# Register loads once a unit, an earlier dst fetch, and 50 instead of 43 double groups gathered singly in a graph-network kernel

## The chip, the cores and the metric

The kernel runs on one core of one Trainium2 chip. A core has five engines with queues of their own: TensorE (PE, matmuls and their weight loads, PEld), VectorE (DVE), ScalarE (ACT), GpSimd (POOL) and SyncE (SP, which here only issues DMAs). Work on one engine runs in order; engines wait for each other by semaphores. The metric is the device time of one execution in microseconds (us).

## The reference

A graph with 12,500 nodes of 128 features and 400,000 edges with 32 features, sorted by destination. With `h = relu(layernorm(x))`, every edge computes a message from its source, its destination and its own features; the messages are summed per destination, and a GRU cell makes the new node:

```
h   = relu(layernorm(x))
m   = relu([h[src], h[dst], ea] @ w1 + b1) @ w2 + b2      # per edge
agg = segment_sum(m, dst)                                 # per node
gi, gh = agg @ w_ih + b_ih, h @ w_hh + b_hh
r, z = sigmoid(gi_r + gh_r), sigmoid(gi_z + gh_z)
n   = tanh(gi_n + r * gh_n)
out = x + (1 - z) * n + z * h
```

## The kernel before

A first stage (to about 120 us) normalizes all nodes. It leaves `hT_all`, h transposed, 128 features by 12,500 nodes, in SBUF, and `A = h @ w1[0:128]`, one row of 512 bytes per node, in DRAM.

The main loop goes over the edges. 128 edges are a tile, eight tiles a *double group* (k, 391 of them), four tiles, a half of it, a *unit* (u, 782 of them). For a unit the pre-activation is a sum of three parts:

- the edge features and the destination: one matmul per two tiles, `pre` (L592), whose weights are a tile `L` of 64 rows of edge features and 64 rows of a one-hot matrix of the destinations, and whose moving side `RW` holds w1's last rows and a window of 2 x 32 destination rows;
- the source: rows `A[src]`, gathered into `G` by one indirect DMA per tile on POOL (L146), and added by DVE (`add`, L617).

Then ACT applies relu into one of three buffers `RB` (L623), and PE sums the edges by destination (`seg`, L636) through a one-hot `OH` of the destinations. `take` brings the sums from PSUM to SBUF on DVE (`sums`, L644) and ACT (`dcol`, L645). Every 14 double groups a block of 512 nodes goes through the GRU (`node`), a generator whose steps are spread over the following units.

The one-hot in `L` is made by DVE (`onehot_T`, L495) from `Ld`, destination numbers that SP's DMA broadcasts over 64 partitions. `fetch(q)` (L479) asks for the edge features and the destinations of two double groups with three DMAs; in the loop it is called two such fetches ahead. `window(k)` copies the destination window out of `hT_all` (`hw`, L514, DVE) at an address from a register, and multiplies it with w1's middle rows (L517, PE); `window_rows` adds b1 into `RW` (L526, DVE).

Some double groups are not gathered by POOL but *singly*, by a job that is spread over many units beforehand (`mode`, `order`, `SPREAD`): 18 by DVE and 19 by ACT, which copy one column of `hT_all` per edge into a tile `HE` (1024 columns a job; L790 and L788), and 6 by SP, which issues one row DMA of 512 bytes per edge (L795). A column's address stands in a register, so an instruction that loads 32 registers from the index list `at` (L782) stands on the same engine before each 32 columns or rows. A double group of DVE's or ACT's has no gathered rows of A: PE multiplies its columns by w1's first rows (L603), and `add` does nothing for it. `G` has seven buffers for POOL's gathers; a gather into a buffer waits until the last reader of that buffer is done.

The order is written by hand. The loop over units issues, for unit u: the gathers that are due, the fetches, `other(0)`, `take`, `stages(u)` (among them `pre(u+3)`, `add(u+2)`, `relu(u+2)`), `other(1)`, `other(2)`, `seg(u)`, `other(3)`. `other(phase)` runs a share of the live jobs (`run_jobs`), in phase 1 of an even unit `window(k+3)`, in phase 3 `window_rows(k+3)` and a step of `node`. A job is a generator: `run_jobs` takes as many steps (4 columns, or 2 rows) as are due by the share of its span that has passed, and a load comes wherever 32 are used up, so its place among the other instructions changes from unit to unit. The jobs of an engine follow each other: the first starts at unit 30, and each ends a few units before its double group is used.

Of the kernel before, what the change touches and what calls it, by code (L numbers as in the profile page):

```python
# [8 lines left out]
F32 = mybir.dt.float32  # L9
# [12 lines left out]
GRP = 4  # L22
# [5 lines left out]
V = 32  # L28
# [14 lines left out]
PLACE = 20  # L43
CH = PLACE * PAIR
LOAD = 32
STEP = {"act": 4, "dve": 4, "sp": 2}
SPREAD = {"act": 19, "dve": 18, "sp": 6}
NR = 12672

H_AT = 16512  # L50
# [6 lines left out]
def tile_gnn(ctx: ExitStack, tc: tile.TileContext, x, src, srcT, dstT, dstP, eaT, eaP, w1, b1, w2T, b2,  # L57
# [26 lines left out]

    mode, order = {}, {m: [] for m in SPREAD}
    for m, n in SPREAD.items():
        lo = JOBS0 + 15
        for i in range(n):
            k = lo + int((i + 0.5) * (NP - 2 - lo) / n)
            while k in mode:  # L90
                k += 1
            mode[k] = m
            order[m].append(k)
# [385 lines left out]
    def fetch(q):  # L479
        if q * QP >= NP:  # L480
            return
        n = min(QP, NP - q * QP)
        Ls[q] = p3.tile([128, QP * 512], F32, name="L")
        c = slice(q * QP * 512, (q * QP + n) * 512)
        nc.sync.dma_start(Ls[q][2 * V:, :n * 512], eaP[:, c])
        Ds[q] = p3.tile([2 * V, QP * 512], I32, name="Ld")
        for a in range(2):
            nc.sync.dma_start(Ds[q][V * a:V * (a + 1), :n * 512],
                              dstP[a:a + 1, c].to_broadcast([V, n * 512]))

    def onehot_T(k):
        if k >= NP:
            return
        c = slice((k % QP) * 512, (k % QP + 1) * 512)
        nc.vector.tensor_scalar(Ls[k // QP][:2 * V, c], Ds[k // QP][:, c], node_of[:, k:k + 1],  # L495
                                None, op0=ALU.is_equal)


    bases, PB_ = {}, {}

    def window(k):
        if k >= NP:
            return
        b = k // BP
        if k % BP == 0:
            n = min(BP, NP - k)
            _, vals = nc.values_load_multi_w_load_instructions(
                base_i[0:1, b, 0:n], engines=[ET.DVE], min_val=0, max_val=LAST,
                skip_runtime_bounds_check_because="clamped above")
            for i, v in enumerate(vals):  # L510
                bases[k + i] = v
        hw = p3.tile([128, 2, V], F32, name="hw", bufs=2)
        s = hT_all[:, bass.ds(bases.pop(k), V + SHIFT)]
        nc.vector.tensor_copy(hw, bass.AP(tensor=s.tensor, offset=s.offset,  # L514
                                          ap=[list(s.ap[0]), [SHIFT, 2], [1, V]]))
        PB_[k] = ps2.tile([128, 512], F32, name="oh")
        nc.tensor.matmul(PB_[k][:2 * V, :D], hw.rearrange("p a v -> p (a v)"), w1b,  # L517
                         start=True, stop=True)

    def window_rows(k):  # L520
        if k >= NP:
            return
        pm = PB_.pop(k)
        for a in range(2):
            s = slice(V * a, V * (a + 1))
            nc.vector.tensor_tensor(RW[k % 4][s, a, :], pm[s, :D], b1b[s, :], op=ALU.add)  # L526
# [80 lines left out]
    def add(u):  # L607
        if u >= NU:
            return
        if u in HE or u // 2 in hand:  # L610
            RT[u] = PP.pop(u)
            HE.pop(u, None)
            if u % 2:
                hand.pop(u // 2, None)
        else:
            RT[u] = unit(u)
            nc.vector.tensor_tensor(RT[u], PP.pop(u), RT[u], op=ALU.add)  # L617

    def relu(u):
        if u >= NU:  # L620
            return
        o = RB[u % 3]
        nc.scalar.activation(o[:, :, :D], RT.pop(u), AF.Relu)  # L623
        if u % 2:
            G.pop(u // 2, None)
# [142 lines left out]
        nc.sync.dma_start(at[r:r + 1, :], src[t0 * 128:(t0 + PAIR) * 128].rearrange(  # L768
            "(o e) -> o e", o=1))

    def one_by_one(m, k):
        et = {"act": ET.Activation, "dve": ET.DVE, "sp": ET.SP}[m]
        r = by_hand.index(k)
        if m == "sp":
            G[k] = pj[0].tile([128, GRP, 2, D], F32, name="G_sp", bufs=1)
            rows = G[k].bitcast(U8)
        else:
            hand[k] = pj[0].tile([128, PAIR * 128], F32, name=f"HE_{m}")
            he = hand[k].bitcast(U8)
        for e0 in range(0, PAIR * 128, LOAD):  # L780
            low, high = (0, ROW * (N - 1)) if m == "sp" else (H_AT, H_AT + 4 * (N - 1))
            _, vals = nc.values_load_multi_w_load_instructions(  # L782
                at[r:r + 1, e0:e0 + LOAD], engines=[et], min_val=low, max_val=high,
                skip_runtime_bounds_check_because="src holds numbers of nodes")
            for i, v in enumerate(vals):
                e = e0 + i
                if m == "act":
                    nc.scalar.copy(he[:, e * 4:e * 4 + 4], h_bytes[:, bass.ds(v - H_AT, 4)])  # L788
                elif m == "dve":
                    nc.vector.tensor_reduce(he[:, e * 4:e * 4 + 4],  # L790
                                            h_bytes[:, bass.ds(v - H_AT, 4), None],
                                            AX.X, ALU.max)
                else:
                    a, j = divmod(e // 128, GRP)
                    nc.sync.dma_start(rows[e % 128:e % 128 + 1, j, a, :],  # L795
                                      A_bytes[bass.ds(v, ROW)].rearrange("(o f) -> o f", o=1))
                if i % STEP[m] == STEP[m] - 1:
                    yield


    jobs = {}
    for m, kl in order.items():
        start = 2 * JOBS0
        for k in kl:
            end = 2 * k - (8 if m == "sp" else 4)
            jobs.setdefault(start, []).append((m, k, end - start))
            start = end if m != "sp" else 2 * k + 2
    live = {}

    PH = 4  # L810

    def run_jobs(u, phase):
        if u == 2 * JOBS0 and phase == 0:
            early.close()
            pj.append(late.enter_context(tc.tile_pool(name="pj", bufs=2, side="right")))
        if phase == 0:
            for m, k, span in jobs.get(u, ()):
                live[m] = [one_by_one(m, k), u, span, PAIR * 128 // STEP[m], 0]
        for m, job in list(live.items()):
            it, start, span, steps, done = job  # L820
            want = -(-steps * ((u - start) * PH + phase + 1) // (span * PH))
            while job[4] < want:
                job[4] += 1
                if next(it, "end") == "end":
                    del live[m]
                    break


    asked = [RAW]
# [9 lines left out]

    gathers(0)  # L840
    for q in range(2):
        fetch(q)
    for k in range(3):
        window(k)
        window_rows(k)


    def stages(u):
        if u + 7 >= 0:
            raw_stats(u + 7)  # L850
        if u + 6 >= 0:
            raw_fin(u + 6)
            raw_h(u + 6)
        if u % 2 == 0:
            onehot_T(u // 2 + 3)
        elif u > -7:
            onehot(u // 2 + 3)
        if u + 4 >= 0:
            raw_turn(u + 4)
        if u + 3 >= 0:  # L860
            pre(u + 3)
        if u + 2 >= 0:
            add(u + 2)
            relu(u + 2)

    for u in range(-7, 0):
        stages(u)
# [12 lines left out]
    for u in range(NU):  # L880
        k, h = divmod(u, 2)
        gathers(u)
        if h == 0:
            if k % QP == 0:
                fetch(k // QP + 2)
            if k % BP == 0 and k:
                nodes_left.append([node(k // BP - 1), 0])
            if k % PLACE == 1:
                indices(k // PLACE + 2)
            if k % PLACE == 5:  # L890
                place(k // PLACE + 1)
                dst_tile(k // PLACE + 2)
            if k == NP - 20:
                check_windows()
        for r in range(2 * u, min(2 * u + 2, NJ)):
            job_indices(r)
        if u == 2 * JOBS0 - 2:
            nc.vector.tensor_scalar(at, at, place_of[:, 0:1], place_of[:, 1:2],
                                    op0=ALU.mult, op1=ALU.add)

        def other(phase):
            run_jobs(u, phase)
            if h == 0 and phase == 1:
                window(k + 3)
            if h == 0 and phase == 3:
                window_rows(k + 3)
            if phase == 3:
                step(nodes_left)

        other(0)  # L910
        if h == 0:
            take(k - 1)
        stages(u)
        other(1)
        other(2)
        seg(u)
        if u == 0:
            node_setup()
        other(3)
# [173 lines left out]
```

## Time and profile before

| what | value |
|---|---|
| median of 3 runs | 3710.21 us (3707.43 to 3713.02) |
| the profiled execution | 3701.45 us, its span 3699.7 us |
| granted TensorE clock, mean | 0.779 |
| POOL gathers | 2781, 958 ns from A, 0.30 us between |
| DVE columns and register loads | 18,432 and 576 |
| ACT columns and register loads | 19,456 and 608 |
| SP rows and register loads | 6,144 and 192 |
| chain that ended last | the last node block alone, from 3692.57 us on |

A group's line gives the source line, the engine, the operation, the tile written and the tile read, how often it ran, its busy time, the mean ns of one, and then the idle time of the engine just before it, with what ended that idle time. "issue" means that no wait is shown: the engine's own sequencer had not yet handed over the instruction. Register loads, semaphore instructions and the issuing of DMAs run on the sequencers and are not in the busy time. A line of stretches gives the stretch, its length, busy us and count for PE, PEld, DVE, ACT and POOL, then the granted clock, the busy share of the DMA engines and GB/s. A line of waits gives the waiting engine, tile and line, what it waited for, the us in total, the times, and the longest. In a timeline a line is a run of like instructions: start, length, engine, line, what, how many, and in brackets the idle time before the first.

### The profile page before, as it was taken

The numbers are of one execution on the slowest core, as the hardware profiler recorded it, in microseconds if no ns is written. First come the engines' busy times: TensorE is split into PE (matmuls) and PEld (weight loads), VectorE is DVE, ScalarE is ACT, GpSimd is POOL, SyncE is SP. The second block draws the span as 40 slices with busy tenths as digits, with TensorE's granted clock in tenths as the row PEclk, the third lists the DMA queues.
The fourth block names the chain that finished last, engine by engine and source line by source line (L and its number), as shares of the span: only waits on it lengthen the run. The fifth ranks groups of instructions, "written<-read, shape, count | busy, mean of one in ns | idle before, by whom it ended". The sixth has DMA issues, their size and how long they took to land. (4 is left out here: it accounts for less than half of the span.)

```text
span 3699.7 us, 94893 instructions
## 1 busy us (share of the span) xinstructions
PE 2649.8 (72%) x13578; PEld 1639.6 (44%) x13578; DVE 2627.5 (71%) x22515; ACT 2513.9 (68%) x20936; POOL 2663.7 (72%) x2789
## 2 busy tenths in 40 slices
PE   6685665667776777677677777766776777677768
PEld 6453333444443444344444444444444444344435
DVE  7765556677777677767777776777777777777774
ACT  5455556677677777767776776777777777777772
POOL 7677646477777677777777777777777677777775
PEclk9897777778787777778777877878777778787779
DMA  6333222233333333333333333333333333333332
GB/s 202 83 91 82 75 66 75 72 90 85 89 85 90 81 87 88 86 86 87 88 91 83 91 87 88 83 90 87 89 88 94 80 92 88 88 89 87 88 87 65
DMA packets 157886, 325.92 MB, mean 88 GB/s; under 512 B 65057, under 2 KB 77132, under 8 KB 157255
## 3 DMA queue, kind: packets, MB, share of 16 engines
q0 software_dynamic: 88992, 182.43, 19.5%
q1 hardware_dynamic: 68119, 137.33, 13.7%
q14 instruction: 519, 4.25, 0.4%
q8 instruction: 112, 1.84, 0.2%
q10 hardware_dynamic: 144, 0.07, 0.0%
HBM read 305.74 MB, written 13.84 MB: 86 GB/s over the span
## 5 line engine op out<-in xcount | busy, mean ns | idle before, releaser
L146 POOL DMA_INDIRECT G<-A,src_i x2704 | 2589.9, 958 | 980.1 <-issue 770.2
L788 ACT COPY HE_act<-hT_all 128x4 uint8 x19456 | 1966.1, 189 | 583.2 <-issue 580.6
L790 DVE TENSOR_REDUCE HE_dve<-hT_all 128x4 uint8 x18432 | 1336.4, 146 | 716.0 <-issue 707.4
L592 PE MATMUL pre<-RW,L 128*128 128x256 f32 x3128 | 1151.4, 497 | 129.8 <-DVE G L617 95.7
L592 PEld LDWEIGHTS pre<-RW,L 128*128 128x128 f32 x3128 | 685.8, 243 | 439.0 <-issue 287.0
L517 PE MATMUL oh<-w1b,hw 128*64 128x128 f32 x782 | 209.4, 358 | 875.7 <-DVE hw L514 862.5
L636 PE MATMUL seg<-RB,OH 128*32 128x129 f32 x6250 | 645.4, 341 | 0.0
L623 ACT ACTIVATE RB<-G 128x512 f32<-128x512 f32 x676 | 424.7, 628 | 323.2 <-DVE G L617 85.2
L517 PEld LDWEIGHTS oh<-w1b,hw 128*64 128x64 f32 x782 | 89.7, 162 | 1030.2 <-DVE hw L514 997.1
L617 DVE TENSOR_TENSOR G<-pre,G 128x512 f32<-128x512 f32 x676 | 461.0, 682 | 10.1 <-PE pre L592 0.3
L636 PEld LDWEIGHTS seg<-RB,OH 128*32 128x32 f32 x6250 | 351.0, 131 | 239.3 <-issue 134.4
L526 DVE TENSOR_TENSOR RW<-oh,b1b 32x128 f32<-32x128 f32 x782 | 217.7, 278 | 48.2 <-PE oh L517 39.8
L495 DVE TENSOR_SCALAR L<-Ld,node_of 64x512 f32<-64x512 int32 x391 | 192.4, 492 | 83.3 <-DMA Ld<-in_dstP 69.5
L544 DVE TENSOR_TENSOR OH<-dloc,iota 128x256 f32<-128x256 f16 (+1 forms) x392 | 162.4, 415 | 0.5 <-issue 0.2
L644 DVE COPY sums<-seg 64x128 f32<-64x128 f32 x391 | 107.4, 275 | 73.2 <-PE seg L636 69.2
L667 PEld LDWEIGHTS nd<-spot,sums 64*128 64x128 f32 x782 | 150.4, 296 | 13.1 <-issue 13.1
L667 PE MATMUL nd<-spot,sums 64*128 64x40 f32 x782 | 154.5, 381 | 0.0
L645 ACT CAST dcol<-seg 64x1 f16<-64x1 f32 x391 | 59.3, 152 | 132.9 <-DVE sums L644 132.3
L631 PE MATMUL seg<-zrow 1*64 1x129 bf16 x391 | 105.8, 271 | 0.0
L514 DVE COPY hw<-hT_all 128x64 f32 x391 | 84.5, 216 | 10.8 <-issue 8.1
L146 POOL DMA_INDIRECT G<-in_x,src_i x77 | 72.9, 946 | 24.9 <-issue 22.9
L631 PEld LDWEIGHTS <-zrow 1*64 1x64 bf16 x391 | 43.2, 110 | 92.2 <-issue 92.2
(151 smaller groups left out, 1511.0 us busy)
## 6 DMA issues: line engine op xcount, KB each, us to landing
G_sp<-A SPq DMA_DIRECT2D x6144, 0.5 KB
L<-in_eaP SPq DMA_DIRECT2D x195, 256.0 KB
Ld<-in_dstP SPq DMA_DIRECT2D x390, 128.0 KB
G<-A,src_i POOLq DMA_INDIRECT x2704
xb<-in_x SPq DMA_DIRECT2D x28, 256.0 KB
out<-xb SPq DMA_DIRECT2D x28, 256.0 KB
xs<-in_x SPq DMA_DIRECT2D x11, 512.0 KB
A<-asb SPq DMA_DIRECT2D x11, 512.0 KB
```

The source lines that it names most:

```text
L146: nc.gpsimd.indirect_dma_start(out=G[k][:, j, a, :], out_offset=None, in_=table, in_offset=bass.IndirectOffsetOnAxis(ap=src_i[c][:, i:i + ...
L495: nc.vector.tensor_scalar(Ls[k // QP][:2 * V, c], Ds[k // QP][:, c], node_of[:, k:k + 1], None, op0=ALU.is_equal)
L517: nc.tensor.matmul(PB_[k][:2 * V, :D], hw.rearrange("p a v -> p (a v)"), w1b, start=True, stop=True)
L526: nc.vector.tensor_tensor(RW[k % 4][s, a, :], pm[s, :D], b1b[s, :], op=ALU.add)
L544: nc.vector.tensor_tensor(o, d.to_broadcast(shape), i.to_broadcast(shape), op=ALU.is_equal)
L592: nc.tensor.matmul(PP[u][:, 2 * i:2 * i + 2, :], Ls[k // QP][:, c0:c0 + 128], RW[k % 4], start=True, stop=not raw)
L617: nc.vector.tensor_tensor(RT[u], PP.pop(u), RT[u], op=ALU.add)
L623: nc.scalar.activation(o[:, :, :D], RT.pop(u), AF.Relu)
L636: nc.tensor.matmul(SEG[k][V * a:V * (a + 1), :D + 1], OH[k][:, j, a, :], RB[u % 3][:, (j % 2) * 2 + a, :D + 1], start=False, stop=all(b != ...
L667: nc.tensor.matmul(pt[:, bass.ds(offs[i], V + SHIFT)], sums[:, i, :], spot, start=False, stop=i == n - 1)
L788: nc.scalar.copy(he[:, e * 4:e * 4 + 4], h_bytes[:, bass.ds(v - H_AT, 4)])
L790: nc.vector.tensor_reduce(he[:, e * 4:e * 4 + 4], h_bytes[:, bass.ds(v - H_AT, 4), None], AX.X, ALU.max)
```

## The change

Five things change together.

- `Job` replaces the generator `one_by_one`, for the three engines. For DVE and ACT, `behind(m, u)` is called once a unit, for DVE right after `add(u+2)`, for ACT right after `relu(u+2)`: it issues the columns left of the registers loaded before, then one load of as many registers as are due until the next unit (30 to 32). Until then `run_jobs` issues the unit's columns in four phases, in the order 1, 2, 3, 0, and holds back the last nine (`TAIL`). So nine columns stand between the long operation and the next load.
- `SPREAD` goes from 18, 19 and 6 double groups (DVE, ACT, SP) to 22, 22 and 6, and their places are spaced anew: DVE's from 34 to 377, ACT's from 42 to 385, SP's at 80, 140, 200, 260, 320 and 381. DVE's first job starts at unit 31, ACT's at 47, SP's at 30. SP's first job has 122 units for its rows, where it had 80; its later ones have 110, as before.
- `fetch` is split. The destinations (`fetch_d`) are fetched three fetches ahead instead of two, and stand before the edge features on SP's queue.
- `window(k)` is split. The copy `hw` moves from phase 1 into `stages`, between the one-hot and `add`; its matmul (`window_b`) stays in phase 1.
- SP's job is cut by rows instead of steps of two rows.

With them the counts on the engines become: DVE 22,528 columns and 719 loads, 662 adds into `G` instead of 676; ACT 22,528 columns and 719 loads; POOL 2725 gathers; SP 6144 rows and 192 loads as before.

```diff
-STEP = {"act": 4, "dve": 4, "sp": 2}
-SPREAD = {"act": 19, "dve": 18, "sp": 6}
+TAIL = 9
+SPREAD = {"dve": 22, "act": 22, "sp": 6}
...
     for m, n in SPREAD.items():
-        lo = JOBS0 + 15
+        lo, hi = {"dve": (JOBS0 + 3, NP - 14), "act": (JOBS0 + 11, NP - 6),
+                  "sp": (JOBS0 + 5, NP - 10)}[m]
         for i in range(n):
-            k = lo + int((i + 0.5) * (NP - 2 - lo) / n)
+            k = lo + int((i + 1) * (hi - lo) / n)
...
         n = min(QP, NP - q * QP)
+        c = slice(q * QP * 512, (q * QP + n) * 512)
         Ls[q] = p3.tile([128, QP * 512], F32, name="L")
+        nc.sync.dma_start(Ls[q][2 * V:, :n * 512], eaP[:, c])
+
+    def fetch_d(q):
+        if q * QP >= NP:
+            return
+        n = min(QP, NP - q * QP)
         c = slice(q * QP * 512, (q * QP + n) * 512)
-        nc.sync.dma_start(Ls[q][2 * V:, :n * 512], eaP[:, c])
         Ds[q] = p3.tile([2 * V, QP * 512], I32, name="Ld")
...
+        HW[k] = hw
+
+    def window_b(k):
+        if k >= NP:
+            return
         PB_[k] = ps2.tile([128, 512], F32, name="oh")
-        nc.tensor.matmul(PB_[k][:2 * V, :D], hw.rearrange("p a v -> p (a v)"), w1b,
+        nc.tensor.matmul(PB_[k][:2 * V, :D], HW.pop(k).rearrange("p a v -> p (a v)"), w1b,
                          start=True, stop=True)
...
+    class Job:
...
+        def load(self, n):
+            m = self.m
             low, high = (0, ROW * (N - 1)) if m == "sp" else (H_AT, H_AT + 4 * (N - 1))
+            et = {"act": ET.Activation, "dve": ET.DVE, "sp": ET.SP}[m]
             _, vals = nc.values_load_multi_w_load_instructions(
-                at[r:r + 1, e0:e0 + LOAD], engines=[et], min_val=low, max_val=high,
+                at[self.r:self.r + 1, self.loaded:self.loaded + n], engines=[et],
+                min_val=low, max_val=high,
                 skip_runtime_bounds_check_because="src holds numbers of nodes")
-            for i, v in enumerate(vals):
-                e = e0 + i
+            self.vals = list(vals)
+            self.loaded += n
+
+        def run(self, left=0):
+            while len(self.vals) > left:
+                v, e, m, to = self.vals.pop(0), self.e, self.m, self.to
+                self.e += 1
                 if m == "act":
-                    nc.scalar.copy(he[:, e * 4:e * 4 + 4], h_bytes[:, bass.ds(v - H_AT, 4)])
+                    nc.scalar.copy(to[:, e * 4:e * 4 + 4], h_bytes[:, bass.ds(v - H_AT, 4)])
...
+    def behind(m, u):
+        if m in live:
+            live[m].run()
+            if live[m].e == PAIR * 128:
+                del live[m]
+        begin(m, u + 1)
+        if m in live:
+            j = live[m]
+            n = PAIR * 128 * (u + 2 - j.start) // j.span - j.loaded
+            assert 0 < n <= LOAD, n
+            j.load(n)
+
+    PARTS = (1, 2, 3, 0)
...
+        for m in ("act", "dve"):
+            if m in live:
+                n = max(0, len(live[m].vals) - TAIL)
+                live[m].run(TAIL + n - -(-n // (4 - PARTS.index(phase))))
         if phase == 0:
-            for m, k, span in jobs.get(u, ()):
-                live[m] = [one_by_one(m, k), u, span, PAIR * 128 // STEP[m], 0]
-        for m, job in list(live.items()):
...
+            begin("sp", u)
...
     for q in range(2):
+        fetch_d(q)
         fetch(q)
+    fetch_d(2)
...
         if u % 2 == 0:
             onehot_T(u // 2 + 3)
+            if u >= 0:
+                window(u // 2 + 3)
...
             add(u + 2)
+            behind("dve", u)
             relu(u + 2)
+            behind("act", u)
...
             if k % QP == 0:
+                fetch_d(k // QP + 3)
                 fetch(k // QP + 2)
...
             if h == 0 and phase == 1:
-                window(k + 3)
+                window_b(k + 3)
```

More of the change, by code (lines that the diff above doesn't have):

```diff
@@ L496, in onehot_T @@
                                 None, op0=ALU.is_equal)
-    bases, PB_ = {}, {}
+    bases, PB_, HW = {}, {}, {}
     def window(k):
@@ L769, in job_indices, with __init__ @@
             "(o e) -> o e", o=1))
[L771 to L780, printed above, removed]
+    class Job:
+        def __init__(self, m, k, start, span):
+            self.m, self.k, self.start, self.span = m, k, start, span
+            self.e, self.loaded, self.vals = 0, 0, []
+            self.r = by_hand.index(k)
+            if m == "sp":
+                G[k] = pj[0].tile([128, GRP, 2, D], F32, name="G_sp", bufs=1)
+                self.to = G[k].bitcast(U8)
+            else:
+                hand[k] = pj[0].tile([128, PAIR * 128], F32, name=f"HE_{m}")
+                self.to = hand[k].bitcast(U8)
+        def load(self, n):
+            m = self.m
             low, high = (0, ROW * (N - 1)) if m == "sp" else (H_AT, H_AT + 4 * (N - 1))
+            et = {"act": ET.Activation, "dve": ET.DVE, "sp": ET.SP}[m]
             _, vals = nc.values_load_multi_w_load_instructions(
-                at[r:r + 1, e0:e0 + LOAD], engines=[et], min_val=low, max_val=high,
+                at[self.r:self.r + 1, self.loaded:self.loaded + n], engines=[et],
+                min_val=low, max_val=high,
                 skip_runtime_bounds_check_because="src holds numbers of nodes")
-            for i, v in enumerate(vals):
-                e = e0 + i
+            self.vals = list(vals)
[4 more added lines that the diff above has]
+                self.e += 1
                 if m == "act":
-                    nc.scalar.copy(he[:, e * 4:e * 4 + 4], h_bytes[:, bass.ds(v - H_AT, 4)])
+                    nc.scalar.copy(to[:, e * 4:e * 4 + 4], h_bytes[:, bass.ds(v - H_AT, 4)])
                 elif m == "dve":
-                    nc.vector.tensor_reduce(he[:, e * 4:e * 4 + 4],
+                    nc.vector.tensor_reduce(to[:, e * 4:e * 4 + 4],
                                             h_bytes[:, bass.ds(v - H_AT, 4), None],
@@ L794, in one_by_one, with begin @@
                     a, j = divmod(e // 128, GRP)
-                    nc.sync.dma_start(rows[e % 128:e % 128 + 1, j, a, :],
+                    nc.sync.dma_start(to[e % 128:e % 128 + 1, j, a, :],
                                       A_bytes[bass.ds(v, ROW)].rearrange("(o f) -> o f", o=1))
-                if i % STEP[m] == STEP[m] - 1:
-                    yield
-    jobs = {}
+    starts = {}
     for m, kl in order.items():
-        start = 2 * JOBS0
+        start = 2 * JOBS0 + (m != "sp") + (16 if m == "act" else 0)
         for k in kl:
             end = 2 * k - (8 if m == "sp" else 4)
-            jobs.setdefault(start, []).append((m, k, end - start))
+            starts[m, start] = (k, end - start)
             start = end if m != "sp" else 2 * k + 2
     live = {}
-    PH = 4
+    def begin(m, u):
+        if (m, u) in starts:
+            live[m] = Job(m, starts[m, u][0], u, starts[m, u][1])
+    def behind(m, u):
[10 more added lines that the diff above has]
+    PARTS = (1, 2, 3, 0)
     def run_jobs(u, phase):
@@ L815, in run_jobs @@
             pj.append(late.enter_context(tc.tile_pool(name="pj", bufs=2, side="right")))
+        for m in ("act", "dve"):
+            if m in live:
+                n = max(0, len(live[m].vals) - TAIL)
+                live[m].run(TAIL + n - -(-n // (4 - PARTS.index(phase))))
         if phase == 0:
-            for m, k, span in jobs.get(u, ()):
-                live[m] = [one_by_one(m, k), u, span, PAIR * 128 // STEP[m], 0]
-        for m, job in list(live.items()):
[L820 to L826, printed above, removed]
+            begin("sp", u)
+        if "sp" in live:
+            j = live["sp"]
+            want = -(-PAIR * 128 * ((u - j.start) * 4 + phase + 1) // (j.span * 4))
+            while j.e < want:
+                if not j.vals:
+                    j.load(LOAD)
+                j.run(max(0, len(j.vals) - (want - j.e)))
+            if j.e == PAIR * 128:
+                del live["sp"]
     asked = [RAW]
@@ L841, in tile_gnn @@
     for q in range(2):
+        fetch_d(q)
         fetch(q)
+    fetch_d(2)
     for k in range(3):
         window(k)
+        window_b(k)
         window_rows(k)
```

## Prediction

> **What bounds the kernel now.** I read the page's totals first, then the busy time by stretches, then the waits of VectorE (DVE), then the order of time around single register loads. The totals:
>
> ```profile
> PE 2649.8 (72%) x13578; PEld 1639.6 (44%) x13578; DVE 2627.5 (71%) x22515; ACT 2513.9 (68%) x20936; POOL 2663.7 (72%) x2789
> L146 POOL DMA_INDIRECT G<-A,src_i x2704 | 2589.9, 958 | 980.1 <-issue 770.2
> L788 ACT COPY HE_act<-hT_all 128x4 uint8 x19456 | 1966.1, 189 | 583.2 <-issue 580.6
> L790 DVE TENSOR_REDUCE HE_dve<-hT_all 128x4 uint8 x18432 | 1336.4, 146 | 716.0 <-issue 707.4
> ```
>
> Four engines look alike, and none is full. But each has idle time ended by "issue". For POOL that is the 0.30 us before every gather: a gather costs 1.26 us from start to start, 2781 x 1.258 = 3497 of the 3699.7 us. For DVE and ACT it is the register load, whose own records are these (counts, and min/median/max in ns):
>
> ```profile
> L782 ACTq TENSOR_LOAD <-at x608: 1966/1992/2536, 226.0 to 3597.6; - x152
> L782 DVEq TENSOR_LOAD <-at x576: 2095/2119/2715, 231.3 to 3603.0; - x192
> ```
>
> 707.4 / 576 = 1.23 us of DVE and 580.6 / 608 = 0.95 us of ACT stand still per load. The stretches (first where SP's first job runs, then the steady part) and DVE's waits in the steady part and in the first one:
>
> ```profile
> 235.00:665.00 430.00, 251.94 (x1248) 148.14 (x1247) 256.91 (x2243) 245.70 (x2068) 284.04 (x299) 0.74 0.29 75
> 860.00:3600.00 2740.00, 1998.85 (x10085) 1215.70 (x10084) 2009.42 (x18067) 1998.68 (x17355) 2035.50 (x2126) 0.77 0.34 88
> ```
>
> ```profile
> DVE HE_dve L790 <- issue: 589.8, 487, 2.7
> DVE TOT L652 <- PE nd L667: 44.9, 17, 3.3
> DVE sums L644 <- PE seg L636: 42.0, 32, 4.0
> DVE RW L526 <- PE oh L517: 12.8, 26, 1.8
> ```
>
> ```profile
> DVE HE_dve L790 <- issue: 79.8, 64, 1.8
> DVE L L495 <- DMA Ld<-in_dstP: 69.5, 14, 7.6
> DVE L L495 <- DMA G_sp<-A: 13.8, 3, 9.0
> ```
>
> In the steady 2740 us 604 units run, 4.54 us each. DVE is busy 2009 and stalled on loads 590: 2599 of 2740, 95%, 4.30 us a unit, and the rest is mostly short waits for PE. POOL's gathers there need 2126 x 1.258 = 2675, 98%; it waits only 68 us for buffers. So DVE and POOL set the pace together, with ACT (1999 + 500 of issue, 4.14 us a unit) just behind. In the first stretch the pace is another: DVE waits 83.3 us for dst tiles, because SP, between 224 and 695 us, issues 1000 single rows with the fetches queued among them, 0.47 us a row, and 12.8 rows a unit are asked of it.
>
> **The change on DVE, the path that sets the end.** Its jobs go from 18 to 22, so columns from 18,432 to 22,528. What a column and a load cost shows here:
>
> ```profile
> 2068.19 0.41 DVE L544 TENSOR_TENSOR OH<-dloc,iota 128x256 f32<-128x256 f16 x1
> 2068.63 0.69 DVE L617 TENSOR_TENSOR G<-pre,G 128x512 f32<-128x512 f32 x1
> 2069.24 1.10 DVE L790 TENSOR_REDUCE HE_dve<-hT_all 128x4 uint8 x16
> 2071.79 0.54 DVE L790 TENSOR_REDUCE HE_dve<-hT_all 128x4 uint8 x7 [1.44 <-issue]
> ```
>
> ```profile
> 2059.55 0.69 DVE L617 TENSOR_TENSOR G<-pre,G 128x512 f32<-128x512 f32 x1
> 2060.16 0.34 DVE L790 TENSOR_REDUCE HE_dve<-hT_all 128x4 uint8 x4
> 2061.75 0.86 DVE L790 TENSOR_REDUCE HE_dve<-hT_all 128x4 uint8 x12 [1.25 <-issue]
> ```
>
> - Columns overlap: 16 in 1.10 us with the last lasting 0.146, so (1.10 - 0.146) / 15 = 0.0636 us each. 4096 more: +260 us.
> - The load. Its record ends 0.08 us before the next column. In the first excerpt it therefore began near 2069.61, when 6 of 16 columns had started and 10 had not: the sequencer runs at most ten instructions ahead. In the second it began with the add (2061.75 - 0.08 - 2.10 = 2059.57), though only four columns stood between. The new order puts exactly the add and nine columns ahead of each load. If the load begins with the add, as it does in 61 of the 66 loads that have four columns behind the add, five more columns take 5 x 0.0636 off 1.25: 0.93 us of stall. In even units the hw copy (0.10) now stands right before the add; a load that begins with it stalls 0.87. In the 88 of 719 units that feed a hand pair there is no add: 0.61 us of cover less, of which the 0.39 of the one-hot before it may come back; about 1.14. Mean 0.88 x 0.90 + 0.12 x 1.14 = 0.93. One load a unit is 719 loads of 30 to 32 values: 719 x 0.93 = 669 against 707: -38. Bounds: 0.76 if a load may always begin one instruction before the add (the OH ahead of it gives 0.39 more in odd units): 546; 0.98 if the loads with eight columns behind the add, which stall 0.96, are the better guide: 705. I take 0.93, from the pattern nearest to the new one.
> - Seven fewer pairs go through an add: 14 x 0.61 = -8.5.
> - dst is asked for one double group earlier, and ahead of L. SP's first job now has 122 units instead of 80, 8.4 rows a unit; at 0.47 us, fetches included, that is 3.9 us a unit, under the unit. So the 83.3 us of waiting for Ld go. Later jobs keep their 110 units and were not late. What is late next there is DVE itself.
> - The window copy moves ahead of the add; its matmul stays in phase 1, where it waits for the copy (PE waited 862.5 us for hw in all). PE gets hw earlier by an add and eight columns, 1.1 us, so seg, the node matmuls and the RW rows behind that matmul come earlier. DVE's waits for PE after 235 us are some 140; more work a unit on DVE gives PE more time as well. I take 60 away; bounds 0 and 120. The base_i load (1.32 us, 28 times) now stands between one-hot and copy, about as exposed as before: nothing, at most 28 x 1 us either way.
>
> Sum against the profiled execution's own 3701.45: +260 - 38 - 8.5 - 83 - 60 = 3772. The median of the runs is 8.8 us above that execution, so 3781.
>
> **What is hidden beside it.** POOL loses 56 gathers, 70 us; it then needs 2725 x 1.258 + 3 at the head + 30 at the tail = 3460, which DVE covers. ACT gains 3072 columns of 0.095 us (24 in 2.38): +292; its loads stalled 0.73 with eight columns behind the activation (90 loads), so 0.63 with nine: 719 x 0.63 = 453 for 582. Net +163, 0.23 us a unit: 4.37, under DVE's 4.76 (4.54 + 0.36 - 0.05 - 0.01 - 0.08). If DVE were below 4.4, ACT would show next. Its copies stand behind the relu, so a longer ACT delays seg by up to the three RB buffers, not at once. PE gets 56 more w1a passes of 0.18 us, 10 us, on an engine that is 27% idle. SP issues the same 6144 rows and 192 loads.
>
> [...]
>
> **The rivals.**
> - The loads hide better (faster). If the sequencer passes the waiting add in both parities, 0.76 us a load, and PE's waits fall by 120: 3781 - 123 - 60 = 3598. For it: 45 loads directly behind an add began before that add started. Against: the 61 with four columns between did not. It decides where the stall falls under 0.83 us: 719 x 0.10 = 71, which brings 3781 to 3710.
> - POOL becomes the bound (faster still): if DVE and ACT both fall under POOL's share, 3460 plus some 40 of buffer waits, 3500. DVE's 4096 columns alone speak against it.
> - The nine columns cover nothing (slower still): 1.25 a load as with four, 719 x 1.25 = 899, and PE's waits stay: 3781 + 230 + 60 = 4070; half of that, 3920, is likelier.
> - Nothing moves: gains and costs cancel within 0.2%, which is about what a measurement of this kernel can tell from no change.
>
> **How the numbers follow.** Forecast 0.58 (its own range 3718 to 3850), better hiding 0.26, POOL 0.05, worse cover 0.07, nothing 0.04. Faster is 0.26 + 0.05 and a little of the forecast's edge, 0.32; same 0.04; slower 0.64. The range takes the better hiding to its value and the worse cover to 3880: stall 0.98 (+36) and PE's waits unchanged (+60) on 3781 give 3877. That is 3600 to 3880.
>
> **What the profile after would show.** Right: DVE's issue idle before its columns near 670 us over 719 loads, Ld waits near nothing, DVE over 97% busy or stalled in the steady part, some 4.75 us a unit, POOL's waits for RB grown from 157 to 300 or more. Wrong: issue idle under 600, or POOL at its 1.26 us without gaps; or ACT's waits for DVE gone, which would make ACT the bound.

## The result, and the profile after

The changed kernel took 5026.52 us (median of four runs, 5022.31 to 5030.89) where the kernel before took 3711.61 (3707.43 to 3717.18): a ratio of 1.354, 95% interval 1.352 to 1.357. The forecast, 3780 us in a range of 3600 to 3880, had the direction and missed the size by 1246 us. The profiled execution of the changed kernel has a span of 5025.4 us (3699.7 before).

The page of the changed kernel, its totals and its three costliest groups (busy time, mean ns, then the idle time before and what ended most of it):

```profile
PE 2968.4 (59%) x13690; PEld 1796.7 (36%) x13690; DVE 2885.5 (57%) x26597; ACT 2809.7 (56%) x24008; POOL 2608.0 (52%) x2733
...
L148 POOL DMA_INDIRECT G<-A,src_i x2648 | 2534.0, 957 | 2324.4 <-ACT RB L636 1523.7
L814 ACT COPY HE_act<-hT_all 128x4 uint8 x22528 | 2280.3, 189 | 1404.3 <-issue 1403.2
L816 DVE TENSOR_REDUCE HE_dve<-hT_all 128x4 uint8 x22528 | 1607.5, 146 | 1584.0 <-issue 1578.0
```

No engine is busy for 60% of the span. The work grew as planned: VectorE's busy time by 258 us. But its columns waited 1578 us for "issue", where 669 were predicted and 707 stood before; ScalarE's waited 1403, where 453 were predicted. POOL, which gathers for everybody, stood 1524 us because RB buffers came free late.

"Issue" in front of a column is the register load: on VectorE its record ends 0.09 us before the next column starts (0.08 before). Its records in the trace of the changed kernel (ns: min/median/max), to be set against 1966/1992/2536 and 2095/2119/2715 before:

```profile
L801 DVEq TENSOR_LOAD <-at x719: 2097/2157/7749, 228.8 to 4829.1; - x180
L801 ACTq TENSOR_LOAD <-at x719: 1967/2023/7313, 368.3 to 4955.2; - x180
```

The medians are the old ones, the maxima are almost three times larger. Two neighbouring units of VectorE, from the timeline (start, time, operation, and in brackets the idle time before it):

```profile
427.37 0.69 DVE L630 TENSOR_TENSOR G<-pre,G 128x512 f32<-128x512 f32 x1
427.97 0.66 DVE L816 TENSOR_REDUCE HE_dve<-hT_all 128x4 uint8 x9
434.79 1.50 DVE L816 TENSOR_REDUCE HE_dve<-hT_all 128x4 uint8 x22 [6.16 <-issue]
...
436.92 0.68 DVE L630 TENSOR_TENSOR G<-pre,G 128x512 f32<-128x512 f32 x1
437.52 0.65 DVE L816 TENSOR_REDUCE HE_dve<-hT_all 128x4 uint8 x9
439.26 1.18 DVE L816 TENSOR_REDUCE HE_dve<-hT_all 128x4 uint8 x17 [1.09 <-issue]
```

Same code, same nine columns behind the add, and a stop of 6.16 us in one unit and of 1.09 in the next. When every load of the trace is put beside the instruction in the program that caused it, one property separates the two kinds: at which index of its list the load starts (modulo four; an index has 4 bytes). Number of loads and median us on each engine, ScalarE's share in the counts alike:

```
values   start mod 4   loads    VectorE us   ScalarE us
32       0             449      2.12         2.02
31       0              22      2.67         2.41
31       1, 2, 3        38      7.12-7.34    6.68-6.70
30       0              56      2.34         2.23
30       1, 2, 3       154      6.77         6.64
```

Before, all loads of 32 started at multiples of 32. In the changed kernel a job of 33 or 34 units takes 30 or 31 values in almost every unit, so about seven in ten of its loads start beside a multiple of four: 192 of 719 on each engine. On VectorE these 192 stopped the columns for 5.61 us each, 1077 us, and the other 527 for 0.946 each, 499 us. Together they are all but 2 us of the 1578 on the page. They lie in 8 of the 22 jobs, so the slowness comes in waves. Two stretches of 200 us of the changed kernel side by side (busy us of PE, PEld, DVE, ACT, POOL with their instructions, then granted clock, DMA share, GB/s):

```profile
1600.00:1800.00 200.00, 110.27 (x478) 65.00 (x478) 104.00 (x1006) 92.37 (x814) 85.10 (x90) 0.65 0.20 52
1800.00:2000.00 200.00, 119.35 (x561) 71.14 (x561) 127.34 (x1237) 135.63 (x1215) 113.98 (x118) 0.65 0.26 68
```

All five engines do less in the first one, 90 gathers for 118: the chain from add to activation to free buffer is stopped as a whole.

### The profile page after: what moved, and what is told of

Read it like the earlier page. It is cut to its first block, busy times and chain, and to the rows that moved or that the text cites. A ratio compares the mean times of both kernels' runs of the same rounds, so it can differ in the third digit from the quotient of the medians.

```text
span 5025.4 us, 102793 instructions
## 1 busy us (share of the span) xinstructions
PE 2968.4 (59%) x13690; PEld 1796.7 (36%) x13690; DVE 2885.5 (57%) x26597; ACT 2809.7 (56%) x24008; POOL 2608.0 (52%) x2733
## 3 DMA queue, kind: packets, MB, share of 16 engines
q8 instruction: 114, 1.87, 0.2%
## 5 line engine op out<-in xcount | busy, mean ns | idle before, releaser
L148 POOL DMA_INDIRECT G<-A,src_i x2648 | 2534.0, 957 | 2324.4 <-ACT RB L636 1523.7
L814 ACT COPY HE_act<-hT_all 128x4 uint8 x22528 | 2280.3, 189 | 1404.3 <-issue 1403.2
L816 DVE TENSOR_REDUCE HE_dve<-hT_all 128x4 uint8 x22528 | 1607.5, 146 | 1584.0 <-issue 1578.0
L605 PE MATMUL pre<-RW,L 128*128 128x256 f32 x3128 | 1306.9, 553 | 620.3 <-DVE G L630 405.6
L605 PEld LDWEIGHTS pre<-RW,L 128*128 128x128 f32 x3128 | 762.9, 270 | 980.5 <-issue 588.4
L530 PE MATMUL oh<-w1b,hw 128*64 128x128 f32 x782 | 230.2, 389 | 1093.7 <-DVE hw L522 1088.8
L649 PE MATMUL seg<-RB,OH 128*32 128x129 f32 x6250 | 695.8, 362 | 108.4 <-ACT RB L636 108.2
L649 PEld LDWEIGHTS seg<-RB,OH 128*32 128x32 f32 x6250 | 373.0, 138 | 468.5 <-ACT RB L636 222.9
L630 DVE TENSOR_TENSOR G<-pre,G 128x512 f32<-128x512 f32 x662 | 452.3, 683 | 10.8 <-issue 0.4
L699 PE MATMUL nd<-DEG,brow 33*128 33x512 f32 x112 | 84.7, 845 | 63.7 <-ACT gt L712 62.5
```

The source lines that it names most:

```text
L148: nc.gpsimd.indirect_dma_start(out=G[k][:, j, a, :], out_offset=None, in_=table, in_offset=bass.IndirectOffsetOnAxis(ap=src_i[c][:, i:i + ...
L530: nc.tensor.matmul(PB_[k][:2 * V, :D], HW.pop(k).rearrange("p a v -> p (a v)"), w1b, start=True, stop=True)
L605: nc.tensor.matmul(PP[u][:, 2 * i:2 * i + 2, :], Ls[k // QP][:, c0:c0 + 128], RW[k % 4], start=True, stop=not raw)
L649: nc.tensor.matmul(SEG[k][V * a:V * (a + 1), :D + 1], OH[k][:, j, a, :], RB[u % 3][:, (j % 2) * 2 + a, :D + 1], start=False, stop=all(b != ...
L814: nc.scalar.copy(to[:, e * 4:e * 4 + 4], h_bytes[:, bass.ds(v - H_AT, 4)])
L816: nc.vector.tensor_reduce(to[:, e * 4:e * 4 + 4], h_bytes[:, bass.ds(v - H_AT, 4), None], AX.X, ALU.max)
```

## The experiments

**Three kernels for the load itself.** The theory (A) is that a load whose start isn't a multiple of four indices takes its values one by one. Rivals: (B) the place of the load, behind the add and at the same time on two engines; (C) the number of values, 30 or 31 for 32. The first kernel keeps the change and only moves the starts:

```diff
-            n = PAIR * 128 * (u + 2 - j.start) // j.span - j.loaded
+            n = PAIR * 128 * (u + 2 - j.start) // j.span // 4 * 4 - j.loaded
```

> The changed kernel with one edit: the number of indices loaded a unit is rounded so that every load starts at a multiple of four indices (16 bytes). 22 + 22 jobs, one load a unit and the nine columns stay; loads are then of 28 or 32 values. In the profile after, loads of 30 or 31 values that start at such a multiple took 2.3 to 2.7 us on VectorE, all others 6.7 to 7.7. Theory A (the start of the list decides a load's time): no load over 2.8 us, VectorE's issue idle before its columns near 670 us instead of 1578, the kernel at 3780 us, between 3700 and 3850. Theory B (the place behind the add, or VectorE and ScalarE loading at the same moment, makes loads slow): loads of 6.7 us remain and the kernel stays above 4700 us. Theory C (a number of values that is not 32 makes them slow): the loads of 28 still take over 6 us; only about half of the 1250 us above the prediction is gone, 4300 to 4500 us.

Measured: 3725.55 us (3717.16 to 3733.36), a ratio of 1.003 to the kernel before (1.002 to 1.005), 1301 us less than the changed kernel. Its loads and its VectorE columns:

```profile
L801 DVEq TENSOR_LOAD <-at x719: 1847/2114/2743, 226.7 to 3593.1; - x180
L801 ACTq TENSOR_LOAD <-at x719: 1729/1985/2677, 301.8 to 3661.8; - x180
```

```profile
PE 2743.0 (74%) x13690; PEld 1697.3 (46%) x13690; DVE 2884.3 (77%) x26597; ACT 2809.6 (75%) x24008; POOL 2605.6 (70%) x2733
...
L814 ACT COPY HE_act<-hT_all 128x4 uint8 x22528 | 2280.3, 189 | 487.4 <-issue 486.3
L816 DVE TENSOR_REDUCE HE_dve<-hT_all 128x4 uint8 x22528 | 1607.4, 146 | 609.3 <-issue 602.2
```

No load above 2.8 us is left, though the loads stand where they stood, at the same time on both engines (against B), and though 120 of VectorE's 719 now have 28 values (1.87 us each, against C). The second kernel asks the reverse question: the kernel before, nothing of the change, lists moved by one index.

```diff
-    at = const.tile([NJ, PAIR * 128], I32, name="at")
+    at = const.tile([NJ, PAIR * 128 + 4], I32, name="at")
...
-                at[r:r + 1, e0:e0 + LOAD], engines=[et], min_val=low, max_val=high,
+                at[r:r + 1, OFF + e0:OFF + e0 + LOAD], engines=[et], min_val=low, max_val=high,
```

(and the same `OFF` where the list is written and scaled; `OFF = 1`).

> The kernel before, with the lists of indices lying one index (4 bytes) further on in their rows: every load is of 32 values, as before, but starts one past a multiple of four; nothing of the change is in it. Theory A (the start): every load goes from 2.1 us to about 32 x 0.226 = 7.2 us on VectorE and 7.0 on ScalarE; 576 loads x 5.1 us are 2940 us more on VectorE, 608 x 5.0 = 3050 on ScalarE; as the two partly wait for each other, 6500 to 8000 us. Theory C (the number of values): nothing changes, 3711 us. Theory B (the place): nothing changes, 3711 us.

Measured: 6473.62 us, one run. The records of its loads, every one of them of 32 values:

```profile
L783 ACTq TENSOR_LOAD <-at x608: 6891/6946/7634, 226.5 to 6357.7; - x152
L783 DVEq TENSOR_LOAD <-at x576: 7122/7192/7996, 231.5 to 6365.4; - x192
L783 SPq TENSOR_LOAD <-at x192: 6477/6737/6907, 222.5 to 5960.3; - x192
```

7.19 us where 2.12 stood, 0.225 us a value; on VectorE the issue idle before columns went from 707 to 3671 us (expected +2940, measured +2964):

```profile
DVE HE_dve L791 <- issue: 3671.0, 588, 7.8
```

The third kernel is its control, `OFF = 4`:

> The same, with the lists four indices (16 bytes) further on: the control, in which the lists move and the starts stay multiples of four. Theory A in its 16-byte form: 2.1 us a load and 3711 us, within 15. If instead the start has to be a multiple of 32, 64 or 128 bytes: loads of about 7 us and the same time as with one index.

Measured: 3708.78 us, one run, with loads of 2097/2117/2740 ns on VectorE. So a shift of 16 bytes left the loads at 2.12 us, where one of 4 bytes took them to 7.19; these lists needed no coarser grid. Theory A holds from both sides, and B and C are out.

**How much the nine columns cover.** Starts at multiples of four, and `TAIL = 0`:

```diff
-TAIL = 9
+TAIL = 0
```

> As the kernel with starts at multiples of four, but no column is kept back behind the long operation (TAIL 0 for 9): the load stands directly behind the add and the activation. If the nine columns cover the load as the prediction's step has it (the load begins with the add either way), each load stalls VectorE 9 x 0.0636 = 0.57 us more, 719 x 0.57 = +411 us against the kernel with nine: 4190 us at most. If the load begins earlier instead, because no nine instructions stand between, part of it comes back: down to 3900. If the nine columns cover nothing (the rival of the prediction): the same time as with nine, within 30 us.

Measured: 3654.89 us (3653.12 to 3660.89), ratio to before 0.984 (0.982 to 0.987). None of the three expectations held: without the nine columns the kernel is 71 us faster than with them, not slower. The stop a load shrank from 0.84 to 0.74 us (528.4 us of issue idle for 602.2). Then four columns:

> The kernel with starts at multiples of four, 22 + 22 jobs, one load a unit, and four columns kept back behind the add for nine. With none kept back the loads began 0.76 us (median) before the add, with five or six instructions unstarted ahead of them, and stalled VectorE 0.73 us each; with nine they began 0.02 us after it, or 0.37 before, and stalled 0.84. If what counts is how much work the ten unstarted instructions hold (theory), four columns behind the add leave room for the one-hot, the copy and the add, and each column kept back adds 0.0636 us of cover to the start that none has: 0.73 - 4 x 0.0636 = 0.48 us, 719 x 0.48 = 345 for 528; the kernel, at 3655 with none, comes to some 3570 to 3620, and POOL (3461 and its waits) is the floor. If the start moves back by as much as the columns add: 3655 to 3725, between the two kernels.

Measured: 3798.46 us (3794.38 to 3802.89), ratio to before 1.024 (1.022 to 1.026): worse than both, with 679.8 us of issue idle. The timeline of one odd unit with four columns, and of one with nine:

```profile
1766.47 0.69 DVE L630 TENSOR_TENSOR G<-pre,G 128x512 f32<-128x512 f32 x1
1767.08 0.34 DVE L816 TENSOR_REDUCE HE_dve<-hT_all 128x4 uint8 x4
1768.68 0.91 DVE L816 TENSOR_REDUCE HE_dve<-hT_all 128x4 uint8 x12 [1.26 <-issue]
```

```profile
1750.09 0.69 DVE L630 TENSOR_TENSOR G<-pre,G 128x512 f32<-128x512 f32 x1
1750.70 0.66 DVE L816 TENSOR_REDUCE HE_dve<-hT_all 128x4 uint8 x9
1752.31 1.56 DVE L816 TENSOR_REDUCE HE_dve<-hT_all 128x4 uint8 x23 [0.95 <-issue]
```

In odd units the load began 0.02 us after the add had started, with four columns (load at 1766.485) as with nine, and the stop differs by five columns: 1.26 - 0.95 = 0.31, and 5 x 0.0636 = 0.32. That is the prediction's own model. In even units the load began 0.37 us before the add with nine (eleven instructions unstarted), 0.6 to 0.9 before it with four, and with none mostly 0.7 to 1.3 us before it, in both parities. So columns kept back do two things: they add cover, and in odd units they tie the load to the start of the add. In odd units with an add a load stopped VectorE for 0.93 us on the mean with nine columns, 1.22 with four and 0.69 with none; in even units for 0.67, 0.64 and 0.69. The three kernels differ in their odd units, where four columns have the tie and little cover. What holds the load back in odd units as soon as columns stand between isn't settled: the prediction's ten unstarted instructions don't explain it, since with four columns behind the add only those four were unstarted. The trace of before had shown part of this: 128 of its loads stand directly behind an add, every one of them began before the add did, and they stopped VectorE for 0.81 us on the mean, less than the 0.93 that the prediction took.

**What the added columns cost.** Starts at multiples of four, nine columns, and the job counts of before (18 and 19):

```diff
-SPREAD = {"dve": 22, "act": 22, "sp": 6}
+SPREAD = {"dve": 18, "act": 19, "sp": 6}
```

> The kernel with starts at multiples of four and nine columns kept back, but with the job counts of before: 18 on VectorE, 19 on ScalarE (43 pairs by hand instead of 50). It prices the added columns. If VectorE sets the pace of that kernel (3725 us), 4096 columns x 0.0636 = 260 us fall away, and the loads, still one a unit, shrink to some 25 values, about 0.4 us shorter, 719 x 0.4 = 290 more. That would be 3180; POOL then holds: 2781 gathers x 1.258 + 33 = 3531, and some 50 of waits for buffers: 3580, between 3540 and 3640. If VectorE isn't what sets the pace, it stays within 40 of 3725.

**Two short loads a unit.** Starts at multiples of four, 22 and 22 jobs; the load is halved, one half behind the add and one behind the one-hot, which moves to where phase 2 ends. The core of the edit:

```diff
-            n = PAIR * 128 * (u + 2 - j.start) // j.span - j.loaded
-            assert 0 < n <= LOAD, n
+            n = PAIR * 128 * (2 * (u + 1 - j.start) + half + 1) // (2 * j.span) // 4 * 4 - j.loaded
+            assert 0 < n <= 20, n
...
         other(2)
+        hots(u)
+        behind("dve", u, 1)
+        behind("act", u, 1)
         seg(u)
```

> The kernel with starts at multiples of four, 22 + 22 jobs, but two loads of 12 or 16 values a unit instead of one of 28 or 32, each with nine columns ahead of it: one behind the add (and the activation), one behind the one-hot, which moves to a place after phase 2 of the unit. A load of 16 is worth 4 x 0.265 = 1.06 us. Behind the add the cover is 0.68 + 9 x 0.0636 = 1.25 us, so nothing is left; behind the one-hot (0.42 or 0.48) it is 1.0, so some 0.15 is left: VectorE's issue idle falls from 602 to about 719 x 0.15 = 110, ScalarE's from 486 to about 150. VectorE then has 3725 - 490 = 3235 and POOL holds: 2725 x 1.258 + 33 = 3461, and 50 to 100 of waits for buffers: 3540, between 3500 and 3600. If two short loads stall as much as one long one, because what counts is the stop and not its length: no change, 3725 or above.

and with more jobs:

> The same with 25 jobs on VectorE and 24 on ScalarE (loads of 16 to 20 values). POOL loses 5 x 8 gathers x 1.258 = 50 us: 3411 and its waits; VectorE gains 3 x 1024 x 0.0636 = 195 and stands at 3430, ScalarE 2 x 1024 x 0.095 = 195. If POOL holds the kernel with two loads: 3490, 50 less than that kernel; if VectorE does: up to 190 more than it.

**The dst fetch alone**, in the kernel before (`fetch` split as in the change, dst three double groups ahead and in front of L, nothing else):

> The kernel before with one part of the change alone: dst is asked for three double groups ahead instead of two, ahead of L; SP's first job keeps its 80 units. It prices the term of 83 us for waits on Ld. If the earlier request alone takes them: 3711 - 83 = 3628. If SP's 1000 rows in 80 units at 0.47 us are the cause, the queue falls behind all the same and one double group (some 18 us) only delays it: 10 to 30 us less, 3690. If VectorE finds the time taken by something else: 3711.

These four ran on one chip that held everything back: 5425.61, 5496.72, 5812.57 and 5549.92 us, and the kernel before itself 5572.03 (5539.93 to 5583.13). There, idle time ended by "issue" shows before instructions of many kinds, not behind loads alone. In the profile of the kernel with the dst fetch, ScalarE's columns waited so 2493 times, against 602 times in the kernel before on the first chip, while the loads kept their 2.1 us. The additions of `window_rows` into RW, with 48 us of idle time before them in the kernel before, show it too:

```profile
L532 DVE TENSOR_TENSOR RW<-oh,b1b 32x128 f32<-32x128 f32 x782 | 218.3, 279 | 867.7 <-issue 710.0
```

What slowed that chip wasn't looked into. The sizes of these runs, the one with 25 and 24 jobs among them, can't be used for the question, and what 25 and 24 jobs would bring stays open; the other three were run again on a chip where the kernel before took 3711.79 us.

> 18 and 19 jobs with starts at multiples of four again, for the same reason. As written for that run: if VectorE sets the pace, POOL takes over with its 2781 gathers, 3580, between 3540 and 3640; if it doesn't, within 40 of 3725.

Measured: 3574.16 us (3568.45 to 3579.73), ratio 0.963 (0.961 to 0.964), at the 3580 expected. POOL waited 7.0 us for RB there (233.4 with 22 and 22 jobs), and VectorE's adds waited 240.7 us for POOL's gathers, a wait that the kernel with 22 and 22 jobs doesn't have. So the added single work set the pace there, and POOL sets it here. The run takes off 4096 columns of VectorE, 3072 of ScalarE, and shortens the loads (issue idle 424 us for 602 on VectorE, 330 for 486 on ScalarE); which of these is worth how much of the 152 us between the kernels isn't separated.

> The kernel with two loads of 12 or 16 values a unit again, because the chip of its first run held all kernels, the kernel before too, at 5400 to 5800 us, so that its size could not be read there. As written for that run: VectorE's issue idle falls from 602 to some 110, POOL holds, 3540, between 3500 and 3600; or no change from 3725, if the stop counts and not its length.

Measured: 3495.79 us (3493.91 to 3496.52), ratio 0.942 (0.940 to 0.943): faster than the kernel before and the changed one. Its columns and POOL's waits (us, times, longest):

```profile
L814 ACT COPY HE_act<-hT_all 128x4 uint8 x22528 | 2273.6, 190 | 20.2 <-issue 9.3
L816 DVE TENSOR_REDUCE HE_dve<-hT_all 128x4 uint8 x22528 | 1706.5, 145 | 283.9 <-issue 262.8
```

```profile
POOL G L148 <- issue: 761.1, 2496, 0.3
...
POOL G L148 <- ACT RB L636: 10.1, 33, 0.3
```

ScalarE's stops are gone altogether (expected 150), VectorE's fell to 263 (expected 110), and POOL gathers without a gap: the 3461 us that its 2725 gathers need plus 34. So the stop isn't a fixed price of a load: 1438 loads of 1.1 us stopped VectorE less than 719 of 2.1 us. That fits a stop that is the part of a load's length that no work covers, with two covers for two short loads. The same edit moved the one-hot, and that move wasn't run by itself.

> The kernel before with dst asked for three double groups ahead alone, again, for the same reason. As written for that run: 3628 if the earlier request alone takes the 83 us of waits for Ld; 3690 if SP's 80 units for 1000 rows keep the queue late; 3711 if VectorE's time is taken by something else.

Measured: 3682.37 us (3677.34 to 3687.22), ratio 0.992 (0.990 to 0.994), 29 us less; 3690 was the expectation where SP's row rate is the cause. The waits for Ld are gone from VectorE, and between 235 and 720 us others stand in their place. PE's and VectorE's waits in that stretch:

```profile
PE oh L523 <- DVE hw L520: 81.7, 35, 5.1
PE pre L598 <- DMA L<-in_eaP: 73.8, 13, 9.9
```

```profile
DVE sums L650 <- PE seg L642: 61.7, 17, 8.9
```

The late transfer is now L, which stands behind dst on SP's queue, and VectorE waits for PE (61.7 us against 6.4 before in the same stretch).

## Why the prediction was wrong, step by step

- **The load (-38 us): this is the step that failed.** The prediction put every load at the 2.10 us of a load of 32 and wrote "719 loads of 30 to 32 values: 719 x 0.93 = 669". For 192 loads, those that start beside a multiple of four, the stop was 5.61. The term is +871 us (1578 for 707) instead of -38 on VectorE. For the other 527 the 0.93 came out at 0.946, partly by luck: loads of 32 values stopped VectorE for 0.90, those of 30 and 31 for 1.14 and 1.35. With all starts at multiples of four it is 0.84: 0.93 in odd units with an add, as predicted, and 0.67 in even ones, where the prediction had 0.87 (its own terms, 0.93 less the copy's 0.10, give 0.83). Against the kernel with starts at multiples of four, VectorE's issue idle is 976 us longer, its waits of sums for seg 207, those of the node gates for ScalarE 101; together 1284 of the 1300 us between the two spans. The last two are how ScalarE's slow loads may reach VectorE; no run repairs the loads of one engine alone, so its share is argued and not shown.
- **The price could have been bounded from the trace of before.** The loads of base_i there take 14 values, and one of them 13, from rows of 64 bytes: three fours and one or two values over (ns: min/median/max):

```profile
L507 DVEq TENSOR_LOAD <-base_i x28: 1115/1322/1599, 105.9 to 3586.2; - x28
```

  The minimum is the load of 13. One value more costs 0.21 us there, while a load of 32 costs 0.066 a value. Whoever sees that a value can have two prices would have put 30 values at up to 30 x 0.21 = 6.3 us; the runs gave 6.8. The prediction took the row for this load's exposure only, and looked at the number of values and the place of the load, not at where it starts.
- **4096 columns (+260): right.** Between the repaired kernel and the one with 18 jobs the group of columns differs by 261 us of busy time (1607.4 against 1346.5).
- **Fewer adds (-8.5): right**, 461.0 to 452.3 us of busy time.
- **Waits for Ld (-83): right in sum, but the earlier fetch is the smaller part.** They are gone after, and in the repaired kernel VectorE's waits for PE don't grow in their place (next point). The fetch alone is worth 29 us; the rest came with the rest of the change, where SP's first job has 122 units. That part wasn't run by itself.
- **Waits for PE (-60): -39 in the repaired kernel** (170 us before, which the prediction put at some 140, and 131 there, both from 235 us on). The split of the window copy wasn't run by itself.
- **The sum.** With the loads repaired: busy +257, loads -105, Ld -83, PE -39, that is +30; measured +25 between the two spans, and 3725.55 us for the forecast of 3781. The forecast's ledger was a forecast of that kernel. That the change came out slower, as forecast, is luck: the cause was one that the prediction did not have, and without it the change costs 0.3%, where 1.9% was forecast.
- **The rivals.** "The loads hide better" needed a stop under 0.83 us; in the repaired kernel it is 0.84, and 0.74 with no column kept back. "The nine columns cover nothing": refuted for odd units, where each of them covers 0.0636; for even units the load moves with them. "POOL the bound" came with two loads a unit, at 3496 where the prediction said 3500. No rival was "a load can have another price", and that was the case.
- **The ten unstarted instructions.** The prediction read "at most ten" from one excerpt. In the trace of before 573 of VectorE's 576 loads and all 608 of ScalarE's had ten or fewer unstarted ahead of them when they began, and three of VectorE's had eleven. In the changed kernel 284 of VectorE's 719 had eleven; the 252 of them with an add in front of the columns began 0.37 us before it (median).
- **The signs.** Issue idle near 670: wrong, 1578. Ld waits near nothing: right. VectorE over 97% busy or stalled in the steady part: wrong, 91% from 860 to 4900 us (2321 busy and 1361 of issue idle). 4.75 us a unit: wrong, 6.4 there, and 4.66 in the repaired kernel. POOL's waits for RB at 300 or more: 1524, by far beyond.

## What to carry to other kernels

When a change alters which addresses or lengths an instruction gets, its old duration need not be its price (32 values took 2.12 or 7.19 us here): look in the trace for the same instruction with another length, and see whether its time goes by pieces. The register loads here took 0.25 to 0.29 us for each four values from starts at multiples of 16 bytes, and 0.225 for each single one from a start 4 bytes beside them, so the chunks that a formula cut had to be rounded to four: 3726 us for 5027. And a stop may be shortened by giving it more covers: half the load at each of two places, with the one-hot moved, was worth 230 us, where other numbers of columns behind the add were worth some 70 either way.

## What the runs showed of the hardware

- A load of registers from a list in on-chip memory: 2.12 us for 32 values on VectorE (2.0 on ScalarE) from a start at a multiple of 16 bytes, 7.19 (6.95) from 4 bytes beside it; 1.87 for 28, 1.11 for 16, 0.86 for 12. That is 0.25 to 0.29 us for each four, or 0.225 for each one. SyncE's loads changed alike, 2.13 to 6.74.
- A gather on POOL took 957 ns in the changed kernel and 958 before, with 0.305 us to the next in both (median), 1.26 us from start to start. In the kernel with two loads a unit, 2725 of them gave the time within 1% (3461 of 3496 us).
- TensorE's granted clock was lower where the engine stood idle for much more of the span: 0.674 in the changed kernel (PE busy 59%) and 0.630 with lists 4 bytes further on (49%), against 0.75 to 0.79 in the kernels with 72 to 76%, among which the order of the two differs. It is a consequence here: starts at multiples of four brought it from 0.674 to 0.757, and PE from 59% to 74%, with no edit on PE.
- The same program took half as long again on another chip (the kernel before, 5572 us for 3712). The trace from that chip, of the kernel with the dst fetch, has stops before instructions of many kinds. Sizes are ratios to the kernel before on the same chip, or differences between kernels on chips where it took 3711.6 to 3712.6 us.
